# Attention weights by transposes: exponential in transposed form, turned back into PSUM, summed by TensorE

## The chip, the cores and the metric

The kernel runs on one core of one Trainium2 chip. A core has engines that run side by side, each with its own instruction queue, worked off in order: TensorE (PE in the profile; its weight loads are PEld), VectorE (DVE), ScalarE (ACT), GpSimd (POOL) and SyncE (SP). DMA queues move data between DRAM and the on-chip memory SBUF. TensorE writes its results to PSUM, a second on-chip memory [...]. An engine waits for another by a semaphore. The metric is the device time of one execution in microseconds.

## The reference, cut to what matters

Four layers of a graph network over 2048 nodes, 8 batch entries and 128 features, with a sparse adjacency matrix (about 16 neighbours a node). Layers 0 and 1 are attention with 8 heads of 16 features:

```
Q, K, V = (h @ Wq, h @ Wk, h @ Wv) split in heads
scores = einsum('bnhd,bmhd->bhnm', Q, K) / sqrt(16)
scores = where(adj == 0, -inf, scores)
attn = softmax(scores, axis=-1)
x = h + (einsum('bhnm,bmhd->bnhd', attn, V) @ Wo + bo)
x = layer_norm(x); x = layer_norm(x + relu(x @ W1 + b1) @ W2 + b2)
```

Layers 2 and 3 are graph attention with scores `leaky_relu(s_i + s_j)` from two vectors, the same mask and softmax, a residual and a layer norm. All is in fp32.

## The kernel before, in words

The nodes are sorted by their number of neighbours and cut into 16 blocks of 128, one node a partition. Block t has room for `CAPS[t]` neighbours, its slots (30 down to 11, 277 in all). Each layer writes a table to DRAM, one row a node, which holds K and V of all 8 batch entries (2048 floats) in layers 0 and 1. For each slot one indirect DMA of POOL (`gather`, L320) fetches for each of the 128 nodes the row of its neighbour into one of six SBUF buffers `kv`. A chunk is two slots in layers 0 and 1 (some have one), 142 chunks a layer. Node lists that are not full have a mask of -1e30 in `lmask`.

`attention_chunk` (L634) is a generator, and each part up to a `yield` is one step:

1. `kk = kk * q` on VectorE (L642), 2048 elements a partition for two slots.
2. VectorE halves the 128 products of each batch entry by adding halves (L647), once or twice (`2 - k // 2 % 2` times), and TensorE adds up the rest into `pair` (L650) with 8 or 4 fp32 matmuls by the identity, each of which runs as two instructions. ScalarE takes the exponential for each slot with the mask as its bias (L655) and puts the 64 weights of the slot (8 batch entries by 8 heads) into the SBUF tile `w`.
3. `vv = vv * w` on VectorE (L661), again 2048 elements.
4. TensorE transposes the products of each slot and batch entry into the accumulator `acc` in PSUM, adding them over the slots (`add_up`, L622, `turn_into`, L327): 8 transposes a slot.

Block 0 has a folded chunk: nodes with more than 28 neighbours put the rest into lists of other partitions, and a matmul with `merge` brings their share back.

When the weights of a block are all there, `sums` adds them over the slots by a tree of VectorE additions (L467 to L471), takes the minimum and maximum for a check on ranges, and the reciprocal (L480). `scales` spreads and transposes the reciprocals, `outputs` (L680) multiplies `acc` by them, and `attention_tail` (L705), once for each half of the batch, runs the output matrix, layer norms, the two-layer network and the next layer's table rows, mostly on TensorE and ScalarE. `general_path` is for inputs that the check on ranges rejects, and is not run here.

The order is written out by hand in `layers` (L1189): every engine gets its instructions in the order in which the Python code makes them, and the framework adds the semaphores that the data and buffers need. One turn of its loop takes chunk i through steps 1 and 2, and chunk i-2 (taken from the list `weighed`) through step 3 and half of step 4; the other half of step 4 comes at the start of the next turn (the list `added`). Three times in a turn `slot` advances the generators of the tails and of the other threads by one step and lets `fetch` issue gathers for which a buffer is free.

`pair` (L168) is one tile of 128 by 512 fp32, one PSUM bank. In layers 2 and 3 it holds the weights of graph attention, which VectorE writes and reads. `misc()` gives one of three other banks.

Of the kernel before, what the change touches and what calls it, by code (L numbers as in the profile page):

```python
# [46 lines left out]
SEG = 128  # L47
BINS = 64

SUM_MIN, SUM_MAX = 1e-25, 1e30  # L50
SCORE_MAX = 80.0


# [31 lines left out]
def sparse_path(ctx: ExitStack, tc: tile.TileContext, ins: dict, out: bass.AP, flag: bass.AP):  # L85
# [19 lines left out]
    def misc():  # L105
        return pm.tile([P, 512], F32, tag="m", name="m")
# [23 lines left out]
    nc.vector.tensor_reduce(  # L130
        group, ident.rearrange("p (g n) -> p g n", n=MANY), axis=AX.X, op=ALU.add
    )
    eps = const.tile([P, 1], F32, name="eps")
    nc.vector.memset(eps, (EPS / D) ** 0.5)
    iota1 = work.tile([P, N], F16, tag="oT", name="iota1", bufs=1)
# [3 lines left out]

    bufs = [const.tile([P, CHUNK], F32, name=f"kv{i}") for i in range(KVB)]  # L140
    turn = [-1]

    def buffer():
        turn[0] += 1
# [3 lines left out]
    kept = [dram.tile([P, B * P], F32, name=f"kept{t}") for t in range(NT)]  # L148
    perm = const.tile([P, NT], I32, name="perm")
    lists = const.tile([P, sum(CAPS)], I32, name="lists")  # L150
    lmask = const.tile([P, sum(CAPS)], F32, name="lmask")
    first = [sum(CAPS[:t]) for t in range(NT)]

    sorted_lists = const.tile([P, BASE + CAPS[1]], I32, name="sorted_lists")
# [172 lines left out]
    def turn_into(dst, src, start):  # L327
        nc.tensor.matmul(  # L328
            dst, src, ident, start=start, stop=True, is_transpose=True, skip_group_check=True
        )  # L330
# [121 lines left out]
    def folded_sums(w, box):  # L452

        columns = w.shape[-1]
        ps = misc()[:, :columns]
        for i in range(FOLD):
            nc.tensor.matmul(ps, merge, w[:, i, :], start=i == 0, stop=i == FOLD - 1)
        box["folded"] = small.tile([P, columns], F32, tag="folded", name="folded", bufs=1)
        nc.scalar.copy(box["folded"], ps)

    def reciprocal_sums(l, t, w, columns, folded):

        sums = small.tile([P, columns], F32, tag="sums", name="sums")
        n = CAPS[t] if t > 0 else BASE
        if l < 2:

            while n > 2:  # L467
                m = -(-n // 2)
                nc.vector.tensor_add(w[:, : n - m, :], w[:, : n - m, :], w[:, m:n, :])
                n = m  # L470
            nc.vector.tensor_add(sums, w[:, 0, :], w[:, 1, :])  # L471
        else:
            nc.vector.tensor_reduce(
                sums, w[:, :n, :].rearrange("p s c -> p c s"), axis=AX.X, op=ALU.add
            )
        if t == 0:
            nc.vector.tensor_add(sums, sums, folded)
        nc.vector.tensor_reduce(dmin[:, l, t : t + 1], sums, axis=AX.X, op=ALU.min)
        nc.vector.tensor_reduce(dmax[:, l, t : t + 1], sums, axis=AX.X, op=ALU.max)
        nc.vector.reciprocal(sums, sums)  # L480
        return sums
# [140 lines left out]
    def add_up(acc, rows, k, n, folded):  # L622

        for i in range(n):
            for b in range(NB):
# [5 lines left out]
                else:  # L631
                    turn_into(acc[:, b, :], rows[:, i, b, :], k + i == 0 and b % 4 == 0)

    def attention_chunk(l, c):  # L634
        box, t, k, ns = c["box"], c["t"], c["k"], c["ns"]
        if k == 0:
            box["acc"] = pacc.tile([P, NB, P], F32, tag="acc", name="acc")
            box["w"] = work.tile([P, max(CAPS), NB * NH], F32, tag="w", name="w")
        acc, w, q = box["acc"], box["w"], box["qf" if c["folded"] else "q"]
        kv = c["buf"].rearrange("p s (b c) -> p s b c", b=NB)  # L640
        kk = kv[:, :, :, :D]
        nc.vector.tensor_mul(kk, kk, q[:, None].to_broadcast([P, ns, NB, D]))  # L642
        yield
        width = D
        for _ in range(2 - k // 2 % 2):
            width //= 2
            nc.vector.tensor_add(kk[:, :, :, :width], kk[:, :, :, :width], kk[:, :, :, width : 2 * width])  # L647
        sc = pair[:, : ns * NB * NH].rearrange("p (s b h) -> p s b h", b=NB, h=NH)
        for j in range(0, width, NH):
            nc.tensor.matmul(  # L650
                sc, ident, kk[:, :, :, j : j + NH], start=j == 0, stop=j + NH == width
            )
        for i in range(ns):
            at = first[t] + k + i
            nc.scalar.activation(  # L655
                w[:, k + i, :], sc[:, i].rearrange("p b h -> p (b h)"), AF.Exp,
                bias=lmask[:, at : at + 1], scale=1.0,
            )
        yield
        vv = kv[:, :, :, D:].rearrange("p s b (j h) -> p (s b) j h", h=NH)  # L660
        nc.vector.tensor_mul(  # L661
            vv, vv,
            w[:, k : k + ns, :].rearrange("p s (b h) -> p (s b) h", h=NH)[:, :, None, :]
            .to_broadcast([P, ns * NB, HD, NH]),
        )
        yield
        if c["folded"]:
            folded_sums(w[:, BASE:, :], box)
        for i in range(ns):
            add_up(acc, kv[:, i : i + 1, :, D:], k + i, 1, c["folded"])  # L670
            yield

    def sums(l, t, box):
        box["r"] = reciprocal_sums(l, t, box["w"], NB * (NH if l < 2 else 1), box.get("folded"))

    def outputs(l, t, box):
        acc, scale = box["acc"], box["scale"]
# [4 lines left out]
    def scales(l, box):  # L682

        box["scale"] = scale = work.tile([P, NB, P], F32, tag="oT", name="scale", bufs=1)
        if l < 2:
            r = box["r"].rearrange("p (b h) -> p b h", h=NH)
            nc.scalar.copy(
                scale.rearrange("p b (j h) -> p b j h", h=NH),
                r[:, :, None, :].to_broadcast([P, NB, HD, NH]),
            )  # L690
            yield
        for i in range(0, NB, 4):
            pt = misc()
# [123 lines left out]
    def gat_tail(l, t, box):  # L817
# [3 lines left out]
        if l == 2:  # L821
            ns = [work.tile([P, 4, D], F32, tag="n", name="n2") for _ in range(2)]
        else:
            n = work.tile([P, max(CAPS), NB * NH], F32, tag="w", name="n")
            n = n.rearrange("p s c -> p (s c)")[:, : B * D].rearrange("p (b d) -> p b d", d=D)
            ns = [n[:, :4, :], n[:, 4:, :]]
        ys = [None, None]
# [68 lines left out]
    def start():  # L896
# [80 lines left out]
            nc.scalar.activation(junk, src, func, accum_out=dst, **kind)  # L977

        def neighbours(t):
            val = work.tile([P, max(CAPS), NB * NH], F32, tag="w", name="val")  # L980
# [12 lines left out]
            return lambda: total(every, AF.Copy, kept_sum[:, t : t + 1])  # L993
# [187 lines left out]
    def chunk(i):  # L1181
        return every[i] if 0 <= i < len(every) else dict(l=None, k=None, last=False, folded=False)

    def go(c, times=1):

        for _ in range(times if c["l"] is not None else 0):
            next(c["run"], None)

    def layers():  # L1189
        threads.append(first_states((0,)))  # L1190
        drain()
# [6 lines left out]
        weighed, added = [], []  # L1198
        for i in range(len(every) + 2):
            c1, c, n1, n2 = (chunk(i + j) for j in range(-1, 3))  # L1200
            while added:
                c2 = added.pop(0)
                go(c2)
                if c2["last"]:
                    threads.append(tail(c2["l"], c2["t"], c2["box"]))
# [20 lines left out]

            if n1["l"] in (2, 3) and n1["folded"]:
                go(n1)
            if c1["l"] in (2, 3) and c1["last"]:
                sums(c1["l"], c1["t"], c1["box"])  # L1230
                threads.append(scales(c1["l"], c1["box"]))
# [3 lines left out]
            slot()  # L1235
            if c["l"] in (0, 1):
                weighed.append(c)
            while weighed and len(weighed) > (2 if c["l"] in (0, 1) else 0):
                c2 = weighed.pop(0)
                if c2["last"]:  # L1240
                    sums(c2["l"], c2["t"], c2["box"])
                    threads.append(scales(c2["l"], c2["box"]))
                go(c2, 2)
                added.append(c2)
            if c1["l"] in (2, 3):
                go(c1, 2)
                if c1["last"]:
# [533 lines left out]
```

## Time and profile before

| | us |
|---|---|
| median of 3 runs (3017.77 to 3019.6) | 3019.43 |
| the profiled execution | 3168.52 |
| its span | 3166.7 |
| DVE busy | 2748.5 |
| PE busy | 2606.0 |
| POOL busy | 1779.9 |
| ACT busy | 1342.0 |

The profiled execution is longer than the runs without a profile, so what is worked out in its time has to be brought to that of the others. The mean granted clock of TensorE was 0.915 of full speed. Layers 0 and 1 run from about 166 us to 2101 us of the span; ahead of them the lists are made and the first table is written, and after them come layers 2 and 3. A row of a group gives the busy time, the mean length of one instruction, and the idle time of its engine just before, with what ended it. In a timeline the first two columns are start and length in us. A matmul's listed mean contains its latency; as matmuls overlap, busy time divided by their number tells the pace.

### The profile page before, as it was taken

How to read it: one execution, taken by the hardware profiler on the slowest of the kernel's cores; microseconds unless marked ns; L12 is line 12 of the kernel's file. 1: busy time of each engine (PE TensorE's matmuls, PEld its weight loads, DVE VectorE, ACT ScalarE, POOL GpSimd, SP SyncE). 2: the span in 40 equal slices, each digit the busy share in tenths (PEclk: the TensorE clock that was granted, in tenths of full speed). 3: DMA queues.
4: the chain of work that ended last, by engine and by line, in shares of the span. 5: the costliest groups of instructions: out<-in, count | busy, mean ns of one | idle time of the engine just before them, and what ended most of it. 6: DMA issues, size and time to landing. Idle time of an engine off the chain costs nothing. (4 is left out here: it accounts for less than half of the span.)

```text
span 3166.7 us, 52148 instructions
## 1 busy us (share of the span) xinstructions
PE 2606.0 (82%) x19258; PEld 2381.0 (75%) x19258; DVE 2748.5 (87%) x2960; ACT 1342.0 (42%) x4895; POOL 1779.9 (56%) x1296
## 2 busy tenths in 40 slices
PE   4766888888899997888898999986787878687786
PEld 3656777777888886777787888885677777577786
DVE  8898999999999988999999999975787876668876
ACT  3511334444445551333443545553444545144354
POOL 0266677588665545455455455554656554666663
PEclk8988899999999998899999999988878888889888
DMA  8688888888888867788888888866988987899994
GB/s 324 247 336 318 308 295 313 318 324 324 323 337 329 324 275 292 257 332 321 308 318 339 316 336 320 316 220 245 362 323 317 353 305 272 331 335 368 362 360 171
DMA packets 200693, 987.63 MB, mean 312 GB/s; under 512 B 31919, under 2 KB 33713, under 8 KB 128437
## 3 DMA queue, kind: packets, MB, share of 16 engines
q0 software_dynamic: 175024, 890.45, 75.9%
q1 hardware_dynamic: 20502, 75.52, 6.3%
q10 hardware_dynamic: 4904, 18.24, 1.5%
q8 instruction: 155, 2.54, 0.3%
q14 instruction: 108, 0.88, 0.1%
HBM read 937.16 MB, written 91.55 MB: 325 GB/s over the span
## 5 line engine op out<-in xcount | busy, mean ns | idle before, releaser
L321 POOL DMA_INDIRECT kv<-table,lists x955 | 1324.4, 1387 | 922.9 <-PE acc L328 579.8
L328 PE MATMUL acc<-ident,kv 128*128 128x128 f32 x8208 | 1091.4, 287 | 208.9 <-DVE kv L661 93.2
L328 PEld LDWEIGHTS acc<-ident,kv 128*128 128x128 f32 x8208 | 991.1, 149 | 306.1 <-issue 149.9
L642 DVE TENSOR_TENSOR kv<-kv,q 128x2048 f32<-128x2048 f32 (+1 forms) x282 | 629.3, 2232 | 63.5 <-DMA kv<-table,lists 25.4
L661 DVE TENSOR_TENSOR kv<-kv,w 128x2048 f32<-128x2048 f32 (+1 forms) x284 | 632.7, 2228 | 0.0
L650 PE MATMUL pair<-kv,ident 128*128 128x128 f32 (+1 forms) x3344 | 449.4, 286 | 145.7 <-issue 66.3
L650 PEld LDWEIGHTS pair<-kv,ident 128*128 128x128 f32 x3344 | 416.4, 199 | 170.0 <-issue 97.8
L799 DVE TENSOR_TENSOR kv<-kv,pair 128x3584 f32<-128x3584 f32 (+1 forms) x150 | 540.1, 3601 | 2.2 <-issue 0.3
L655 ACT ACTIVATE w<-pair,lmask 128x64 f32<-128x64 f32 x554 | 144.7, 311 | 749.6 <-PE pair L650 736.4
L647 DVE TENSOR_TENSOR kv<-kv 128x1024 f32<-128x1024 f32 (+1 forms) x434 | 442.6, 1020 | 14.4
L496 ACT ACTIVATE n<-m,eps 128x128 f32<-128x128 f32 x512 | 181.4, 367 | 305.4 <-PE m L720 160.3
L321 POOL DMA_INDIRECT kv<-table,sorted_lists x153 | 194.5, 1271 | 131.1 <-PE acc L328 49.0
L846 ACT ACTIVATE n<-m,eps 128x128 f32<-128x128 f32 x256 | 90.7, 372 | 354.4 <-remote 125.7
L804 ACT ACTIVATE kv<-kv,ws 128x128 f32<-128x128 f32 x554 | 176.6, 401 | 86.8 <-issue 29.9
L517 POOL DMA_INDIRECT table<-rows,perm x57 | 80.6, 1414 | 136.9 <-ACT score L570 42.4
L754 PE MATMUL m<-w_L_w,hT 128*128 128x128 f32 x1024 | 156.5, 275 | 0.0
L810 DVE TENSOR_TENSOR kv<-kv 128x1024 f32<-128x1024 f32 x75 | 91.5, 1220 | 73.4 <-ACT kv L804 72.5
L503 ACT ACTIVATE n<-m,rs 128x128 f32<-128x128 f32 x512 | 146.5, 377 | 1.1
L680 DVE TENSOR_TENSOR o<-acc,scale 128x512 f32<-128x512 f32 x128 | 82.9, 684 | 63.7 <-PE acc L328 37.3
L754 PEld LDWEIGHTS m<-w_L_w,hT 128*128 128x128 f32 x1024 | 135.3, 193 | 0.0
L335 PE MATMUL m<-ident,n 128*128 128x128 f32 x640 | 116.1, 303 | 22.6 <-ACT kv L804 6.8
L733 PE MATMUL m<-n1T,w_L_gnn_W 128*128 128x512 f32 x256 | 131.5, 597 | 0.6 <-ACT q L608 0.6
(238 smaller groups left out, 3668.3 us busy)
## 6 DMA issues: line engine op xcount, KB each, us to landing
kept<-xT SPq DMA_DIRECT2D x48, 512.0 KB
xT<-kept SPq DMA_DIRECT2D x48, 512.0 KB
kv<-in_adj_dram SPq DMA_DIRECT2D x16, 1024.0 KB
table<-kv ACTq DMA_DIRECT2D x16, 1024.0 KB
kv<-table,lists POOLq DMA_INDIRECT x955
kv<-in_x_nodes_dram SPq DMA_DIRECT2D x16, 512.0 KB
kv<-table,sorted_lists POOLq DMA_INDIRECT x153
found<-cand POOLq DMA_DIRECT2D x16, 64.0 KB
```

The source lines that it names most:

```text
L321: nc.gpsimd.indirect_dma_start(out=dst, out_offset=None, in_=tables[l][:, :], in_offset=bass.IndirectOffsetOnAxis(ap=index, axis=0), bound ...
L328: nc.tensor.matmul(dst, src, ident, start=start, stop=True, is_transpose=True, skip_group_check=True)
L496: nc.scalar.activation(dst[:, i, :], z[:, i, :], AF.Square, bias=eps, scale=D**-0.5, accum_out=ss[:, i : i + 1],)
L503: nc.scalar.mul(dst[:, i, :], z[:, i, :], rs[:, i : i + 1])
L642: nc.vector.tensor_mul(kk, kk, q[:, None].to_broadcast([P, ns, NB, D]))
L647: nc.vector.tensor_add(kk[:, :, :, :width], kk[:, :, :, :width], kk[:, :, :, width : 2 * width])
L650: nc.tensor.matmul(sc, ident, kk[:, :, :, j : j + NH], start=j == 0, stop=j + NH == width)
L655: nc.scalar.activation(w[:, k + i, :], sc[:, i].rearrange("p b h -> p (b h)"), AF.Exp, bias=lmask[:, at : at + 1], scale=1.0,)
L661: nc.vector.tensor_mul(vv, vv, w[:, k : k + ns, :].rearrange("p s (b h) -> p (s b) h", h=NH)[:, :, None, :] .to_broadcast([P, ns * NB, HD, ...
L754: nc.tensor.matmul(y[:, j, :], hT[:, f, j, :], wt["2"][:, f, :], start=False, stop=f == 1, skip_group_check=True,)
L799: nc.vector.tensor_mul(hv[:, :, :nv, :], hv[:, :, :nv, :], wc[:, :, :nv, None].to_broadcast([P, ns, nv, D]))
L804: nc.scalar.mul(hv[:, i, b, :], hv[:, i, b, :], ws[:, i, b - nv : b - nv + 1])
```

## The change

In layers 0 and 1, VectorE folds once in every chunk, and writes the result by feature, with the 64 columns of both slots side by side, into a tile `hk`. TensorE then adds up eight transposes of `hk` in `pair[:, :128]`, so that a score stands with (slot, batch entry, head) in the partition and the node in the column, and adds the mask, now kept in bf16, with one bf16 matmul a slot. ScalarE takes one exponential of 128 by 128 into `eT`. At the start of the next turn TensorE transposes `eT` back into one of two other parts of `pair`, and the multiplication by V reads the weights from there. The sums of the weights are made by TensorE from the kept exponentials (`block_sums`, for up to eight chunks at a time), and the reciprocal becomes an exponential of the negative logarithm on ScalarE. The bounds of the check on ranges are narrower. The order of the turn has the new step at its start; the lag of two chunks between exponential and multiplication by V stays.

```
-    lmask = const.tile([P, sum(CAPS)], F32, name="lmask")
+    lmask = const.tile([P, sum(CAPS)], BF16, name="lmask")
...
-        if l < 2:
-            while n > 2:
-                m = -(-n // 2)
-                nc.vector.tensor_add(w[:, : n - m, :], w[:, : n - m, :], w[:, m:n, :])
-                n = m
-            nc.vector.tensor_add(sums, w[:, 0, :], w[:, 1, :])
...
+    def block_sums(l, t, box, last):
+
+        terms = [(e, fold_slots[: e.shape[0], :]) for e, folded in box["exps"] if not folded]
+        if "partial" in box:
+            terms.append((ident, box["partial"]))
+        if last and t == 0:
+            terms += [(merge, box["wf"][:, i, :]) for i in range(FOLD)]
+        ps = misc()[:, : NB * NH]
+        for i, (a, b) in enumerate(terms):
+            nc.tensor.matmul(
+                ps, a, b, start=i == 0, stop=i + 1 == len(terms), skip_group_check=True
+            )
+        name = "sums" if last else "partial"
+        box[name] = small.tile([P, NB * NH], F32, tag=name, name=name)
+        nc.scalar.copy(box[name], ps)
+        box["exps"].clear()
+        if last:
+            box["r"] = small.tile([P, NB * NH], F32, tag="logs", name="logs", bufs=1)
+            nc.scalar.activation(box["r"], ps, AF.Ln)
+            threads.append(scales(l, box))
...
-        width = D
-        for _ in range(2 - k // 2 % 2):
-            width //= 2
-            nc.vector.tensor_add(kk[:, :, :, :width], kk[:, :, :, :width], kk[:, :, :, width : 2 * width])
-        sc = pair[:, : ns * NB * NH].rearrange("p (s b h) -> p s b h", b=NB, h=NH)
-        for j in range(0, width, NH):
+        m, at = ns * NB * NH, first[t] + k
+        hk = work.tile([P, NH, P], F32, tag="hk", name="hk")[:, :, :m]
+        kj = kk.rearrange("p s b (j h) -> p (s b) j h", h=NH)
+        nc.vector.tensor_add(
+            hk.rearrange("p j (c h) -> p c j h", h=NH), kj[:, :, :NH, :], kj[:, :, NH:, :]
+        )
+        sc = pair[:m, :P]
+        for j in range(NH):
+            turn_into(sc, hk[:, j, :], j == 0)
+        for i in range(ns):
             nc.tensor.matmul(
-                sc, ident, kk[:, :, :, j : j + NH], start=j == 0, stop=j + NH == width
-            )
-        for i in range(ns):
-            at = first[t] + k + i
-            nc.scalar.activation(
-                w[:, k + i, :], sc[:, i].rearrange("p b h -> p (b h)"), AF.Exp,
-                bias=lmask[:, at : at + 1], scale=1.0,
-            )
+                sc[i * NB * NH : (i + 1) * NB * NH, :],
+                lmask[:, at + i : at + i + 1].to_broadcast([P, NB * NH]), ident_bf,
+                start=False, stop=True, skip_group_check=True,
+            )
+        eT = box["eT"][:m, len(box["exps"]) % NH, :]
+        nc.scalar.activation(eT, sc, AF.Exp)
+        box["exps"].append((eT, c["folded"]))
+        yield
+        turns[0] += 1
+        back = P + turns[0] % 2 * P
+        w = pair[:, back : back + m]
+        nc.tensor.matmul(
+            w, eT, ident[:m, :m], start=True, stop=True, is_transpose=True, skip_group_check=True
+        )
...
+        if c["last"] or len(box["exps"]) == NH:
+            block_sums(l, t, box, c["last"])
         yield
         vv = kv[:, :, :, D:].rearrange("p s b (j h) -> p (s b) j h", h=NH)
         nc.vector.tensor_mul(
             vv, vv,
-            w[:, k : k + ns, :].rearrange("p s (b h) -> p (s b) h", h=NH)[:, :, None, :]
+            w.rearrange("p (s b h) -> p (s b) h", b=NB, h=NH)[:, :, None, :]
             .to_broadcast([P, ns * NB, HD, NH]),
         )
...
-            nc.scalar.copy(
+            nc.scalar.activation(
                 scale.rearrange("p b (j h) -> p b j h", h=NH),
-                r[:, :, None, :].to_broadcast([P, NB, HD, NH]),
+                r[:, :, None, :].to_broadcast([P, NB, HD, NH]), AF.Exp, scale=-1.0,
             )
...
+            for c2 in weighed[-1:]:
+                go(c2)
             while added:
                 c2 = added.pop(0)
                 go(c2)
```

More of the change, by code (lines that the diff above doesn't have):

```diff
@@ L48 @@
 BINS = 64
-SUM_MIN, SUM_MAX = 1e-25, 1e30
+SUM_MIN, SUM_MAX = 1e-15, 1e15
 SCORE_MAX = 80.0
@@ L132, in sparse_path @@
     )
+    fold_slots = const.tile([P, NB * NH], F32, name="fold_slots")
+    nc.vector.tensor_add(fold_slots, ident[:, : NB * NH], ident[:, NB * NH :])
     eps = const.tile([P, 1], F32, name="eps")
@@ L141, in sparse_path @@
     turn = [-1]
+    turns = [0]
     def buffer():
@@ L464, in reciprocal_sums @@
         n = CAPS[t] if t > 0 else BASE
-        if l < 2:
-            while n > 2:
-                m = -(-n // 2)
-                nc.vector.tensor_add(w[:, : n - m, :], w[:, : n - m, :], w[:, m:n, :])
-                n = m
-            nc.vector.tensor_add(sums, w[:, 0, :], w[:, 1, :])
-        else:
-            nc.vector.tensor_reduce(
-                sums, w[:, :n, :].rearrange("p s c -> p c s"), axis=AX.X, op=ALU.add
-            )
+        nc.vector.tensor_reduce(
+            sums, w[:, :n, :].rearrange("p s c -> p c s"), axis=AX.X, op=ALU.add
+        )
         if t == 0:
@@ L637, in attention_chunk @@
             box["acc"] = pacc.tile([P, NB, P], F32, tag="acc", name="acc")
-            box["w"] = work.tile([P, max(CAPS), NB * NH], F32, tag="w", name="w")
-        acc, w, q = box["acc"], box["w"], box["qf" if c["folded"] else "q"]
+            box["eT"] = work.tile([P, NH, P], F32, tag="w", name="eT")
+            box["exps"] = []
+        acc, q = box["acc"], box["qf" if c["folded"] else "q"]
         kv = c["buf"].rearrange("p s (b c) -> p s b c", b=NB)
@@ L643, in attention_chunk @@
         yield
-        width = D
-        for _ in range(2 - k // 2 % 2):
-            width //= 2
-            nc.vector.tensor_add(kk[:, :, :, :width], kk[:, :, :, :width], kk[:, :, :, width : 2 * width])
-        sc = pair[:, : ns * NB * NH].rearrange("p (s b h) -> p s b h", b=NB, h=NH)
-        for j in range(0, width, NH):
+        m, at = ns * NB * NH, first[t] + k
[8 more added lines that the diff above has]
+        for i in range(ns):
             nc.tensor.matmul(
-                sc, ident, kk[:, :, :, j : j + NH], start=j == 0, stop=j + NH == width
-            )
-        for i in range(ns):
-            at = first[t] + k + i
-            nc.scalar.activation(
-                w[:, k + i, :], sc[:, i].rearrange("p b h -> p (b h)"), AF.Exp,
-                bias=lmask[:, at : at + 1], scale=1.0,
-            )
+                sc[i * NB * NH : (i + 1) * NB * NH, :],
+                lmask[:, at + i : at + i + 1].to_broadcast([P, NB * NH]), ident_bf,
+                start=False, stop=True, skip_group_check=True,
+            )
+        eT = box["eT"][:m, len(box["exps"]) % NH, :]
[8 more added lines that the diff above has]
+        )
+        if c["folded"]:
+            box["wf"] = small.tile([P, FOLD, NB * NH], F32, tag="wf", name="wf", bufs=1)
+            nc.scalar.copy(box["wf"].rearrange("p s c -> p (s c)"), w)
+        if c["last"] or len(box["exps"]) == NH:
+            block_sums(l, t, box, c["last"])
         yield
@@ L666, in attention_chunk @@
         yield
-        if c["folded"]:
-            folded_sums(w[:, BASE:, :], box)
         for i in range(ns):
@@ L673, in sums @@
     def sums(l, t, box):
-        box["r"] = reciprocal_sums(l, t, box["w"], NB * (NH if l < 2 else 1), box.get("folded"))
+        if l < 2:
+            nc.vector.tensor_reduce(dmin[:, l, t : t + 1], box["sums"], axis=AX.X, op=ALU.min)
+            nc.vector.tensor_reduce(dmax[:, l, t : t + 1], box["sums"], axis=AX.X, op=ALU.max)
+            return
+        box["r"] = reciprocal_sums(l, t, box["w"], NB, box.get("folded"))
     def outputs(l, t, box):
@@ L823, in gat_tail @@
         else:
-            n = work.tile([P, max(CAPS), NB * NH], F32, tag="w", name="n")
+            n = work.tile([P, NH, P], F32, tag="w", name="n")
             n = n.rearrange("p s c -> p (s c)")[:, : B * D].rearrange("p (b d) -> p b d", d=D)
@@ L979, in neighbours @@
         def neighbours(t):
-            val = work.tile([P, max(CAPS), NB * NH], F32, tag="w", name="val")
+            val = work.tile([P, NH, P], F32, tag="w", name="val")
             val = val.rearrange("p s c -> p (s c)").bitcast(F16)[:, :N]
@@ L1187, in go, with weigh @@
             next(c["run"], None)
+    def weigh(some, added):
+        for c2 in some:
+            if c2["last"]:
+                sums(c2["l"], c2["t"], c2["box"])
+            go(c2, 2)
+            added.append(c2)
     def layers():
@@ L1228, in layers @@
                 go(n1)
+            if c["l"] not in (0, 1) and weighed:
+                weigh(weighed, added)
+                weighed = []
             if c1["l"] in (2, 3) and c1["last"]:
@@ L1237, in layers @@
                 weighed.append(c)
[L1238 to L1244, printed above, removed]
+            if len(weighed) > 2:
+                weigh(weighed[:1], added)
+                weighed.pop(0)
             if c1["l"] in (2, 3):
```

## The prediction

> **What bounds the kernel now.** I began with the page's busy shares and its forty slices, then asked for the busy time of each engine by stage, because layers 0 and 1 (the only ones that run the changed code) may have another limit than layers 2 and 3.
>
> ```profile
> PE 2606.0 (82%) x19258; PEld 2381.0 (75%) x19258; DVE 2748.5 (87%) x2960; ACT 1342.0 (42%) x4895; POOL 1779.9 (56%) x1296
> ...
> DVE  8898999999999988999999999975787876668876
> ```
>
> ```profile
> 166.00:2101.00 1935.00, 1674.32 (x12839) 1538.64 (x12837) 1824.76 (x1504) 809.63 (x2906) 1146.09 (x680) 0.95 0.84 313
> 2101.00:3166.70 1065.70, 824.41 (x5901) 758.16 (x5901) 783.19 (x918) 461.78 (x1825) 604.85 (x579) 0.85 0.86 315
> ```
>
> In the second fence the columns are stage, its length, busy time of PE, PE's weight loads, DVE, ACT and POOL, granted PE clock, DMA share and GB/s. The attention stage lasts 1935 us. DVE is busy 94% of it, PE 87%, DMA 84%: DVE sets the pace, with two others close behind. It handles 284 chunks (142 a layer, 14 of them with one slot, the rest with two), so one takes 6.81 us. The groups of that stage say where DVE's time goes (busy us, mean ns, idle before):
>
> ```profile
> L661 DVE TENSOR_TENSOR kv<-kv,w 128x2048 f32<-128x2048 f32 x270 | 616.5, 2283 | 0.0
> L642 DVE TENSOR_TENSOR kv<-kv,q 128x2048 f32<-128x2048 f32 x268 | 612.3, 2285 | 63.5 <-DMA kv<-table,lists 25.4 <-DMA kv<-table,sorted_lists 16.7 <-ACT q L608 10.1
> L647 DVE TENSOR_TENSOR kv<-kv 128x1024 f32<-128x1024 f32 x270 | 330.5, 1224 | 8.8
> L647 DVE TENSOR_TENSOR kv<-kv 128x512 f32<-128x512 f32 x158 | 109.6, 693 | 5.4
> ```
>
> Idle before the value multiplication L661 is 0.0: DVE never waits for the weights. The timeline shows why:
>
> ```profile
> 305.43 0.69 DVE L647 TENSOR_TENSOR kv<-kv 128x512 f32<-128x512 f32 x1
> ...
> 306.22 1.13 PE L650 MATMUL pair<-kv,ident 128*128 128x128 f32 x8 [1.77 <-ACT rs L487]
> ...
> 306.48 2.28 DVE L661 TENSOR_TENSOR kv<-kv,w 128x2048 f32<-128x2048 f32 x1
> 307.39 0.52 ACT L655 ACTIVATE w<-pair,lmask 128x64 f32<-128x64 f32 x2 [1.79 <-PE pair L650]
> ...
> 308.82 1.97 PE L328 MATMUL acc<-ident,kv 128*128 128x128 f32 x8 [1.47 <-DVE kv L661]
> ...
> 314.81 1.04 PE L328 MATMUL acc<-ident,kv 128*128 128x128 f32 x8
> ```
>
> After the last fold of chunk i, PE adds the scores and ACT takes the exponential, ending at 307.91; yet L661 started at 306.48, because it serves chunk i-2, whose weights lay ready in SBUF. Scores and exponential hang behind DVE, not in its way. The chain of waits says the same from the other side (total us, times, longest):
>
> ```profile
> ACT w L655 <- PE pair L650: 736.4, 276, 12.9
> PE acc L328 <- DVE kv L661: 93.2, 82, 3.2
> ```
>
> [...] the mostly transposing stage of layers 2 and 3 has clock 0.85 at 77% busy, attention 0.95, and the same eight transposes take 1.04 or 1.97 us in the lines above.
>
> **The change part by part.** All in the attention stage; everything else keeps its 3167 - 1935 us.
>
> *DVE loses* the 512 and 256 wide folds (109.6 + 2.5 us), the tree of sums (50.7 + 7.2 + 0.5) and the reciprocal (17.7): 188 us busy, about 175 of time, as consecutive DVE rows overlap by some 80 ns. The remaining fold writes eight-element runs into `hk` at 512-byte steps; no row shows such a write. I take the 1224 ns of L647; [...] at twice that it would add 1.2 us a chunk. Reading `w` from PSUM costs nothing: L799, which reads its weights from `pair`, takes 3887 ns for 3584 elements, the SBUF rate.
>
> *PE* loses L650, 428.0 + 21.3 = 449 us. It gains 284 x 8 score transposes at 132 ns (580.2 us / 4384 of L328) = 300; 554 mask matmuls in bf16, between 50 and 204 ns each (the latter is the mean of the 128x64 bf16 row of `places`), taken as 100 = 55; 284 transposes back = 37; and about 300 fp32 sum matmuls with 64 columns, two instructions each at 121 ns (21.3 us / 176) = 73. That is 465: PE gains nothing.
>
> *ACT*: one 128x128 exponential (377 ns as L503) replaces two of 128x64 (0.52 us together). About 50 copies and logarithms at 0.2 us, and an exponential in place of the copy in `scales`, hide in its idle time (44% busy, and less needed than before); without cover some 20 us. *DMA, POOL, SP*: the same gathers in the same order, no transfer added. Masks in bf16, constants and buffer sizes cost no time.
>
> *The added wait.* `pair` is one PSUM bank. It now holds the scores that PE writes and ACT reads, and beside them the turned-back weights that DVE reads. In the built instruction order L693, the value multiplication of chunk i-2, waits for the ScalarE semaphore value set by the exponential of chunk i, the latest reader of the bank. Two chunks of lag are gone as far as DVE is concerned: K product(i), fold(i), score transposes(i), masks(i), exponential(i), value product(i-2), K product(i+1) are one chain. Behind the waiting L693 stand all of DVE's next chunk, PE's `add_up`, and through it POOL's gathers into that buffer. One two-slot turn of this chain, from the timeline: K product 2.31 (start to start with its fold), fold 1.23, to PE 0.05, eight transposes 1.10, two masks 0.2, to ACT 0.04, exponential 0.37, back to DVE 0.05, value product 2.20: 7.55 us, against 5.67 to 6.38 in the same stretch before. With 14 chunks of about 4.6 the mean is 7.40.
>
> On top come three things. (a) DVE's other work: `outputs` 40.5, minima and maxima 13.7, lists about 35: 0.33 us a chunk, a third of which falls into the new stall; 0.22. (b) PE in its order. After the value product it must do two groups of `add_up` (1.04 each) and the transpose back (0.13), 2.2 us, plus the tail steps recorded between, before the next scores; DVE needs 3.5 for K product and fold, so up to 1.3 us of tail hide. PE's tail work is 1674 - 580 - 449 = 645 us, 20 us a block of 9 chunks, in lumps of up to 3 us (24 matmul instructions of line 754 and 749), in about six of the nine turns. Laying a block's steps over the three slots gives 4 to 9 us of lateness a block, according to the slot where they fall; I take 6.7, or 0.75 a chunk. (c) The clock: with PE less busy and its score matmuls turned into transposes I expect layers 2 and 3's 0.85 rather than 0.95, about 0.6 us on the 5 us of PE in the chain wherever PE binds, which is less than half the time: 0.25.
>
> 7.40 + 0.22 + 0.75 + 0.25 = 8.62 us. 284 x 8.62 = 2448, and about 40 us of DMA and transition waits stay: 2488 for the stage, 553 more than 1935. The profiled execution took 3168.5 us where the median is 3019.4, a ratio of 0.953, which I apply to the difference: +527, 3546 us.
>
> **The rivals.** *R1, the bare chain:* PE keeps up and the clock holds. 7.40 + 0.22 + about 0.2 = 7.8 us; 284 x 7.8 + 40 = 2255, +320, scaled +305: 3325 us. For it: PE falls to 75% busy, so its lateness can drain. Against: the lumps come at fixed places of the order. *R2, a cold PE:* if most transposes run at 1.97 us per eight, `add_up` alone takes 4.2 us after each value product, past DVE's 3.5, and the scores 0.9 more: over 9.4 us a chunk, some 9.6: +831, scaled +792, 3810 us. For it: the 1.97 line after an idle of 1.47. [...] *R3, faster:* the stall is covered and DVE's 175 us count in full: 3019 - 0.953 x 175 = 2853; as PE's 1690 us would then stand in a stage of 1760, up to some 2930. The wait decides unless DVE had over 1.8 us of other work queued between fold and value product in every chunk; it has about 0.1. That the wait does not act at all is the same rival, and it stands in the built order.
>
> **How the numbers follow.** Forecast (8.2 to 9.4 us a chunk, 3430 to 3760 us) 0.52; R1 (below 8.2) 0.28; R2 0.17; R3 0.03, with a sliver at no change. A range of 3290 to 3770 leaves out R3, the lowest fifth of R1 and most of R2. A measurement here tells 0.2% from no change; slower 0.97, faster 0.02, same 0.01.
>
> **What would show it.** Right: idle before the value product L693 of about 2.5 to 3 us a chunk, released by ACT's exponential L677; DVE near 65% busy in the stage; PE busy about as before in a longer stage, at a clock below 0.9; DMA near 245 GB/s there (606 MB in 2488 us); layers 2 and 3 unchanged. Of the terms, (b) shows as ACT waiting for PE's score or mask matmuls later than 1.4 us after the fold's end, and the fold's price in its own row. Wrong: no idle before L693, or a release by an exponential two chunks back; a fold of 2.4 us would put the loss on the strided write instead.

## The result and the profile after

The changed kernel takes 3525.8 us (median of 4 runs, 3525.0 to 3526.6) where the kernel before takes 3019.5 us: a ratio of 1.1675, with a 95% interval of 1.1655 to 1.1695. It is slower by 506 us; forecast were 527.

One thing has to be known to compare the profiles. Layers 2 and 3, which the change does not touch, last about 1050 us in some of the profiles of this study and about 935 us in others, whatever the kernel, and with them the kernel before takes 3141 to 3144 us or 3017 to 3020 us. All runs of a set on one chip agree in it, so it seems to go by the chip; what else ran beside them is not on record, and the cause is open. The profile of the kernel before has the long form (1065 us), the profile of the change the short one (935 us). So kernels are compared by the length of the attention stage, which hardly depends on it (the change has 2419 us in the short form and 2416 in the long one), and by their ratio to the kernel before on the same chip. The kernel before was profiled once, in an execution that is longer than all its 39 others on chips with the long form (3168.5 us, the others at most 3160.9), so its 1931 us of attention may be some 20 us too long.

The page of the changed kernel, busy shares and DVE's slices:

```profile
PE 2759.6 (78%) x19620; PEld 2465.8 (70%) x19620; DVE 2589.0 (73%) x2633; ACT 1295.9 (37%) x4705; POOL 1478.9 (42%) x1296
...
DVE  8877677776766766766666666666667999769997
```

DVE falls to six or seven tenths through the attention slices and comes back to nine only in layers 2 and 3. The attention stage, in the answer by stage (stage, length, busy time of PE, PE's weight loads, DVE, ACT and POOL, PE clock, DMA share, GB/s):

```profile
166.00:2588.00 2422.00, 1893.00 (x13173) 1658.78 (x13174) 1663.11 (x1169) 761.88 (x2710) 846.13 (x684) 0.89 0.70 251
2588.00:3523.00 935.00, 759.85 (x5928) 724.00 (x5927) 784.00 (x920) 462.35 (x1829) 602.53 (x574) 0.89 0.91 357
```

DVE's work fell from 1825 to 1663 us, as the change intends, and its share from 94% to 69%. The time is in its waits. From the groups of the stage (busy us, mean ns, idle before), and last the row of L693 on the page, which takes in the one-slot chunks:

```profile
L693 DVE TENSOR_TENSOR kv<-kv,pair 128x2048 f32<-128x2048 f32 x270 | 617.9, 2288 | 716.8 <-ACT eT L677 714.0 <-PE pair L683 2.7
L659 DVE TENSOR_TENSOR kv<-kv,q 128x2048 f32<-128x2048 f32 x268 | 612.3, 2285 | 2.9 <-DMA kv<-table,lists 2.9
L664 DVE TENSOR_TENSOR hk<-kv 128x1024 f32<-128x1024 f32 x270 | 330.7, 1225 | 8.9
...
L693 DVE TENSOR_TENSOR kv<-kv,pair 128x2048 f32<-128x2048 f32 (+1 forms) x284 | 635.0, 2236 | 743.3 <-ACT eT L677 740.4
```

The value product L693 had no idle time before it; now it has 743 us, released by the exponential L677. The fold with its steps of 512 bytes costs 1225 ns, what the plain one cost, and the product that reads PSUM 2288 against 2283 ns. The timeline of one turn on the three engines, from the K product to the next one:

```profile
812.77 2.28 DVE L659 TENSOR_TENSOR kv<-kv,q 128x2048 f32<-128x2048 f32 x1
...
812.91 1.09 PE L331 MATMUL acc<-ident,kv 128*128 128x128 f32 x8 [2.11 <-DVE kv L693]
...
814.39 1.04 PE L331 MATMUL acc<-ident,kv 128*128 128x128 f32 x8
...
815.09 1.23 DVE L664 TENSOR_TENSOR hk<-kv 128x1024 f32<-128x1024 f32 x1
...
816.38 1.09 PE L331 MATMUL pair<-ident,hk 128*128 128x128 f32 x8 [0.95 <-DVE hk L664]
817.40 0.25 PE L671 MATMUL pair<-ident_bf,lmask 128*64 128x128 bf16 x2
...
817.68 0.28 ACT L677 ACTIVATE eT<-pair 128x128 f32<-128x128 f32 x1 [2.61 <-PE pair L671]
818.00 2.29 DVE L693 TENSOR_TENSOR kv<-kv,pair 128x2048 f32<-128x2048 f32 x1 [1.68 <-ACT eT L677]
...
820.20 2.28 DVE L659 TENSOR_TENSOR kv<-kv,q 128x2048 f32<-128x2048 f32 x1
```

One turn is 820.20 - 812.77 = 7.43 us, each step started by the end of the one before it, on three changes of engine: VectorE to TensorE, TensorE to ScalarE, and ScalarE back to VectorE. This is the bare chain. The waits of the whole program (total us, times, longest) show who stands behind it:

```profile
POOL kv L324 <- PE acc L331: 1289.5, 466, 8.2
ACT eT L677 <- PE pair L671: 818.8, 226, 12.4
DVE kv L693 <- ACT eT L677: 740.4, 280, 7.1
```

PE waits for L693 with its `add_up`, and POOL's gathers wait for PE.

I took the wait apart for each of the 284 chunks, from the times of the trace: from the fold's end to the first score transpose 1.09 us in the mean (median 0.55, a tenth above 2.8), scores and masks 1.35 (1.21 at the shortest), to the exponential 0.07, the exponential 0.28, to the value product 0.07 (median 0.03). The sum is 2.85 us; without PE's lateness, by which is meant the first of these terms, it would be about 1.8. VectorE is idle for 2.62 us of it, as some of its other work falls into this time.

### The profile page after: what moved, and what is told of

It is laid out like the page before. It is cut to its first block, busy times and chain, and to the rows that moved or that the text cites. A ratio compares the mean times of both kernels' runs of the same rounds, so it can differ in the third digit from the quotient of the medians.

```text
span 3523.3 us, 52422 instructions
## 1 busy us (share of the span) xinstructions
PE 2759.6 (78%) x19620; PEld 2465.8 (70%) x19620; DVE 2589.0 (73%) x2633; ACT 1295.9 (37%) x4705; POOL 1478.9 (42%) x1296
## 4 chain that ended last, share of the span: by engine, by line
PE 53%; DVE 22%; DMA 8%; issue 8%; ACT 5%; POOL 0%; POOLq 0%; DVEq 0%; ACTq 0%
PE acc L331 19%; DVE kv L693 10%; PE pair L331 8%; DMA kv<-table,lists 7%; DVE kv L659 5%; PE m L788 3%; DVE hk L664 3%; DVE kv L833 2%; PE m L638 2%; PE m L750 2%; PE m L754 2%; PE m L338 2%; PE m L767 2%; ACT eT L677 2%; PE m L783 2%
## 5 line engine op out<-in xcount | busy, mean ns | idle before, releaser
L324 POOL DMA_INDIRECT kv<-table,lists x955 | 1122.8, 1176 | 1527.2 <-PE acc L331 1199.5
L331 PE MATMUL acc<-ident,kv 128*128 128x128 f32 x8208 | 1170.5, 300 | 527.6 <-DVE kv L693 443.9
L331 PEld LDWEIGHTS acc<-ident,kv 128*128 128x128 f32 x8208 | 1044.9, 156 | 621.5 <-DVE kv L693 506.9
L693 DVE TENSOR_TENSOR kv<-kv,pair 128x2048 f32<-128x2048 f32 (+1 forms) x284 | 635.0, 2236 | 743.3 <-ACT eT L677 740.4
L331 PE MATMUL pair<-ident,hk 128*128 128x128 f32 (+1 forms) x2272 | 330.5, 293 | 68.8 <-DVE hk L664 65.9
L677 ACT ACTIVATE eT<-pair 128x128 f32<-128x128 f32 (+1 forms) x284 | 79.0, 278 | 821.4 <-PE pair L671 818.8
L331 PEld LDWEIGHTS pair<-ident,hk 128*128 128x128 f32 (+1 forms) x2272 | 281.8, 152 | 97.4 <-DVE hk L664 90.6
L664 DVE TENSOR_TENSOR hk<-kv 128x1024 f32<-128x1024 f32 (+1 forms) x284 | 340.4, 1198 | 9.3
L754 PE MATMUL m<-w_L_o,o 128*128 128x128 f32 x512 | 120.2, 324 | 0.0
L772 ACT ACTIVATE hT<-m,w_L_col 128x512 f32<-128x512 f32 x128 | 89.3, 697 | 69.4 <-PE m L767 69.4
```

What stands on the lines that cost most here:

```text
L324: nc.gpsimd.indirect_dma_start(out=dst, out_offset=None, in_=tables[l][:, :], in_offset=bass.IndirectOffsetOnAxis(ap=index, axis=0), bound ...
L331: nc.tensor.matmul(dst, src, ident, start=start, stop=True, is_transpose=True, skip_group_check=True)
L664: nc.vector.tensor_add(hk.rearrange("p j (c h) -> p c j h", h=NH), kj[:, :, :NH, :], kj[:, :, NH:, :])
L693: nc.vector.tensor_mul(vv, vv, w.rearrange("p (s b h) -> p (s b) h", b=NB, h=NH)[:, :, None, :] .to_broadcast([P, ns * NB, HD, NH]),)
L754: nc.tensor.matmul(z[:, j, :], oT[:, j, :], wt["o"], start=False, stop=True, skip_group_check=True)
```

## The experiments

The theory: the value product of chunk i-2 now waits for the exponential of chunk i, because its weights lie in the bank of the scores; this puts scores and exponential into DVE's way. Its rival: the transposes themselves cost the time, through PE's order or its clock. All whole-program medians come with the ratio to the kernel before on the same chip.

**The weights copied to SBUF.** ScalarE copies the turned-back weights, so that VectorE leaves the bank; all else stays.

```
+        ws = small.tile([P, P], F32, tag="wsb", name="wsb", bufs=2)[:, :m]
+        nc.scalar.copy(ws, w)
+        w = ws
```

> The change with one addition: ScalarE copies the turned-back weights from PSUM into SBUF, and the value product reads them there, so VectorE reads nothing in the bank of the scores. Theory (the wait of the value product for the exponential of the chunk two ahead makes the loss): idle before the value product falls from 743 us to under 100, VectorE's 175 us of saved work come through in part, and the whole takes 2860 to 2960 us, less than the kernel before. Rival (the transposes cost the time, through TensorE's order or its clock): 3300 us or more, TensorE's idle turned into lateness of the scores. Rival (the strided write of the fold): no change from 3526, but its row already shows 1225 ns.

It took 3129.8 us, 0.9975 of the kernel before (0.9958 to 0.9992). Attention fell from 2419 to 1906 us. The groups of its stage:

```profile
L696 DVE TENSOR_TENSOR kv<-kv,wsb 128x2048 f32<-128x2048 f32 (+1 forms) x284 | 634.2, 2233 | 34.5 <-ACT wsb L687 30.2 <-ACT rs L481 3.3 <-issue 0.8
L659 DVE TENSOR_TENSOR kv<-kv,q 128x2048 f32<-128x2048 f32 (+1 forms) x282 | 630.3, 2235 | 161.1 <-DMA kv<-table,lists 106.3 <-ACT q L603 30.1 <-DMA kv<-table,sorted_lists 24.1
```

The wait is gone (34.5 us), and with it the whole loss, though every transpose is still there and ScalarE has more to do. The rival falls. The expected gain did not come: 11 us of the whole program by the medians, 26 of attention by the two profiles, where DVE has some 170 us less to do. It now waits 130 us for gathers.

**Another order.** K product, value product of i-2, transpose back of i-1, and then fold and scores; the bank stays shared.

```
-            for c2 in weighed[-1:]:
-                go(c2)
...
             go(c)
+            if len(weighed) > 1:
+                weigh(weighed[:1], added)
+                weighed.pop(0)
+            for c2 in weighed[-1:]:
+                go(c2)
             slot()
             go(c)
...
-            if len(weighed) > 2:
-                weigh(weighed[:1], added)
-                weighed.pop(0)
```

> The change with another order in the turn of attention: K product of chunk i, value product of chunk i-2, then the transpose back of i-1, then fold and scores of chunk i. The bank is still shared and the semaphores still guard it, but the value product now comes a whole K product after the last exponential. Theory of the wait: idle before the value product falls to 50 to 200 us (what is left is TensorE's lateness), total 2880 to 3080 us. Rival that the bank itself slows TensorE or VectorE: 3300 us or more, since all the accesses are still there.

3240.8 us, 1.031 (1.028 to 1.035), where the expectation had a gain or 2% of loss at most; attention 2028 us. From the waits of DVE:

```profile
DVE kv L693 <- ACT eT L677: 313.3, 166, 6.7
```

Four fifths of the loss go by order alone, with all the accesses to the bank in place. The idle time, 337 us with smaller causes, was more than the 200 us expected: the fold's end to the first score transpose takes 1.6 us in the mean here, and what is later than the K product's cover shows.

**The wait alone, in the kernel before.** A copy of one element a partition of the newest exponential, ahead of each value product.

```
+    newest = [None]
...
+        newest[0] = w[:, k + ns - 1, :1]
         yield
         vv = kv[:, :, :, D:].rearrange("p s b (j h) -> p (s b) j h", h=NH)
+        probe = small.tile([P, 1], F32, tag="probe", name="probe")
+        nc.vector.tensor_copy(probe, newest[0])
```

> The kernel before with the wait alone: ahead of each value product VectorE copies one element a partition of the newest exponential, that of the chunk two ahead, and so waits for it. Nothing else of the change is in it. Theory of the wait: the chain of a chunk becomes 2.31 + 1.23 or 1.95 of folds + 1.1 or 1.97 of scores + 0.52 + 2.20 and about 0.3 between, 8.4 us, with VectorE's other work and TensorE's lateness 9.2 to 9.8: 3700 to 3880 us in all, slower than the change itself, whose chain is shorter. Rival that the wait is worth little and the transposes make the loss: under 3200 us.

3773.8 us, 1.2017 (1.1984 to 1.2051), attention 2562 us or 9.02 a chunk, a little under the 9.2 to 9.8 expected.

From the waits:

```profile
DVE probe L664 <- ACT w L656: 666.0, 261, 7.9
```

From the groups:

```profile
L665 DVE TENSOR_TENSOR kv<-kv,w 128x2048 f32<-128x2048 f32 (+1 forms) x284 | 633.2, 2230 | 0.0
```

The product waits for nothing, the copy ahead of it for 666 us. The wait without the change costs as much as the change and more; by the sum in the expectation, this is because two folds and up to sixteen score instructions make the chain longer.

**The change again**, as a base on the chip of the next runs.

> The change itself once more, beside the others on one chip, as a base for them. In the first set the layers 2 and 3 of every kernel took about 1050 us, as in the profile of the kernel before, where the profile of the change had 936 us; the attention stage had 2419 us. Expected: attention 2400 to 2440 us again on whatever chip, as the chain does not depend on DMA there; the whole 3500 to 3540 us if layers 2 and 3 take 936, or 3620 to 3670 us if they take 1050.

3644.7 us, 1.1601 (1.1562 to 1.164); attention 2416 us, layers 2 and 3 1056 us. Attention stays, the rest moves, as expected: what differs between chips is outside the changed stage.

**Where PE's lateness comes from: tail steps moved.** The first slot of the turn, ahead of the scores, is put behind them.

```
             go(c)
-            slot()
+            if c["l"] not in (0, 1):
+                slot()
             go(c)
             slot()
             if c["l"] in (0, 1):
+                slot()
                 weighed.append(c)
```

> The change with the tails' first slot of each attention turn moved from ahead of the scores to behind them, where TensorE has the exponential and the value product (2.6 us) as cover. Theory (1.1 us a chunk beyond the bare chain is TensorE's lateness from tail steps recorded between value product and next scores): a third to a half of these 320 us goes, 3360 to 3430 us. Rival (the time beyond the bare chain is the slower TensorE clock or ScalarE's queue): 3500 us or more.

3617.7 us; attention 2385 us, 31 us less than the change instead of 100 to 160, with the lateness at 1.09 us as before. A miss: two steps in a row can outlast the value product, and `add_up` is late instead. From the value product's end to the first `add_up` transpose it takes 0.71 us in the mean, where the change has 0.35, so the place of the slots mostly moves the lateness.

**The two-layer network left out** of the attention tails of the change; steps and layer norms stay.

```
...
-            nc.tensor.matmul(
-                ph, wt["1"][:, f * P : (f + 1) * P], n1T.rearrange("p b c -> p (b c)"),
-                start=True, stop=True,
-            )
             yield
-            nc.scalar.activation(
-                hT[:, f].rearrange("p b c -> p (b c)"), ph, AF.Relu,
-                bias=wt["col"][:, 4 + f : 5 + f], scale=1.0,
-            )
...
-            for f in range(2):
-                nc.tensor.matmul(
-                    y[:, j, :], hT[:, f, j, :], wt["2"][:, f, :], start=False, stop=f == 1,
-                    skip_group_check=True,
-                )
```

> The change with the two-layer network left out of the attention tails (no W1 and W2 matmuls, no relu; the steps and the layer norms stay), which takes about 280 us of TensorE work out of the attention stage. Theory (the 1.09 us between fold and first score transpose is TensorE still at tail steps): this lateness falls to 0.3 to 0.6 us, the wait of 2.80 us a chunk to 1.9 to 2.3, attention from 2419 to 2200 to 2300 us. Rival (the lateness is the add_up transposes at a slow clock): no fall, or a rise with a lower clock, attention above 2380 us.

Attention 2378 us (3594.0 in all), the lateness 0.93 us: a sixth less, not half. Another miss, and the stage is about as long as the rival had it (above 2380): the granted clock of the stage fell to 0.87, and `add_up`, with the same number of transposes, took 717 us instead of 689. The trace of the change shows what PE does between the end of a value product and the next first score transpose. Of 309 us of lateness in all, 200 lie in 70 chunks that are over 2 us late. In these PE spends 2.2 us on `add_up`, 1.2 on the output projection with its residual (L750, L754), 0.8 on the block sums (L638) and about 0.5 on the two-layer network.

The clock has a part in it. In the trace's record the granted clock is either full or half: in the attention stage of the change it is at half for 543 us (22%), in that of the kernel before for 186 us (10%). The starts of successive `add_up` transposes in the change are about 109 ns apart or, 803 times in 3815, 190 to 240 ns, and 792 of these 803 lie where the record has the half clock. About a fifth of the matmuls in the stretch before the scores follow each other at the doubled distance. As an estimate from these distances, the lateness would be about 0.7 us instead of 1.09 at full pace, and about 0.4 instead of 0.93 with the network left out. So theory and rival both seem to hold in part: with the network left out, PE has 1734 us of work in the stage in place of 1893, and what is left ran slower (`add_up` 717 us for 689). No run tests the clock alone.

**The block sums covered.** The last sums of a block go behind the scores of their turn.

```
-        if c["last"] or len(box["exps"]) == NH:
-            block_sums(l, t, box, c["last"])
+        if not c["last"] and len(box["exps"]) == NH:
+            block_sums(l, t, box, False)
...
             go(c)
+            if c1["l"] in (0, 1) and c1["last"] and "sums" not in c1["box"]:
+                block_sums(c1["l"], c1["t"], c1["box"], True)
             slot()
```

> The change with the last sums of a block (32 of the 48 groups of sum matmuls) moved from the start of the turn to behind the scores of that turn, under the cover of the value product. In the trace of the change these matmuls stand in front of the latest scores (1.0 us of the 3 us and more). Theory that what TensorE does between value product and next scores makes the 1.09 us of lateness, block sums among it: attention 2375 to 2405 us against 2416, lateness 0.95 to 1.05 us. Rival that the sums are harmless there: within 5 us of 2416.

3508.1 us, 1.1628 (1.1601 to 1.1655); attention 2397 us against 2416 to 2419, lateness 1.04. As expected: the sums take part, about 20 us by the 32 groups that moved.

**Where the gain of the copy version goes: two ways to free the buffers earlier.** Both add to the copy version. First a lag of one chunk, with gathers let further ahead.

```
-            if now[1] - now[0] > (4 if now[1] >= KVB and every[now[1] - KVB]["l"] > 1 else 3):
+            if now[1] - now[0] > 4:
...
-            if len(weighed) > 2:
+            if len(weighed) > 1:
```

> The change with the copy to SBUF and with a lag of one chunk in place of two between exponential and value product, and gathers let one chunk further ahead: buffers come free a turn earlier. Theory that the copy version waits for gathers (130 us of idle before the K product) because buffers are held for three turns: these waits fall under 60 us and the whole is 2 to 5% under the kernel before. Rival (TensorE is then late with the weights, as one K product and fold, 3.5 us, must cover add_up, tail steps, transpose back and copy): idle before the value product rises by 150 us or more and the whole is slower than the copy version.

3173.1 us, 1.0108 (1.0064 to 1.0153); attention 1952 us. On the same chip the copy version itself:

> The change with the weights copied to SBUF by ScalarE, once more, as the base of the run with a shorter lag. Theory that DMA now limits it: attention near 1906 us if the chip has the slower layers 2 and 3, and 1780 to 1860 us with a clear gain over the kernel before (2 to 5%) if it has the faster ones.

3124.8 us, 0.9939 (0.991 to 0.9969), attention 1898 us. From the groups of the run with a lag of one:

```profile
L696 DVE TENSOR_TENSOR kv<-kv,wsb 128x2048 f32<-128x2048 f32 (+1 forms) x284 | 635.1, 2236 | 205.7 <-ACT wsb L687 189.5 <-issue 7.0 <-ACT xT L799 3.5
L659 DVE TENSOR_TENSOR kv<-kv,q 128x2048 f32<-128x2048 f32 (+1 forms) x282 | 629.4, 2232 | 11.4 <-DMA kv<-table,lists 8.0 <-issue 2.9 <-DMA kv<-table,sorted_lists 0.5
```

The gathers are in time (11 us), and the weights are late instead (206 us): the rival named ahead holds. Then the lag of two again, with both slots summed in one turn, and from then until the next turn gathers let one chunk further ahead.

```
-            if now[1] - now[0] > (4 if now[1] >= KVB and every[now[1] - KVB]["l"] > 1 else 3):
+            if now[1] - now[0] > (4 if now[1] >= KVB and every[now[1] - KVB]["l"] > 1 else 3 + ahead[0]):
...
-            go(c2, 2)
+            go(c2, 3)
             added.append(c2)
...
+            ahead[0] = 0
...
+                ahead[0] = 1
```

> The change with the copy to SBUF, the lag of two chunks kept, but both slots of a chunk summed into the accumulator in one turn (the second slot's transposes no longer wait for the next turn), and gathers then let one chunk further ahead. It tells whether the copy version's 125 us of waits for gathers come from DMA's rate or from the moment at which a buffer comes free. Free moment: the waits before the K product fall under 60 us, idle before the value product stays under 70 us, the whole is 1.5 to 4% under the kernel before. Rate: the waits stay above 100 us and the whole stays within 0.5 points of the copy version's 0.994 to 0.998.

This came on the chip with the short layers 2 and 3: 3033.9 us against 3017.2, 1.0048 (1.0032 to 1.0063), attention 1932 us, waits for gathers 96 us and for weights 60. Neither expectation fits. Three versions with different lags, leads and chips end at 1898 to 1952 us, and in all of them PE is busy for 1705 to 1724 us. The stage of the copy version, columns as above:

```profile
169.00:2074.00 1905.00, 1705.53 (x13169) 1513.99 (x13170) 1650.26 (x1167) 813.54 (x2992) 1139.37 (x673) 0.96 0.85 316
```

So the next theory was that PE sets their pace.

**PE's work reduced in both kernels.** The two-layer network left out of the copy version and of the kernel before, by the edit shown above.

> The change with the copy to SBUF and without the two-layer network of the attention tails (W1, W2 and the relu left out), some 280 us less of TensorE work in the attention stage. The three copy versions all ended with attention at 1898 to 1952 us, whatever the lag and the gathers' lead, with TensorE 88 to 90% busy. Theory that TensorE, and through its late release of buffers the gathers, now sets their pace, so that VectorE's saved 175 us can't come through: attention falls to 1700 to 1800 us, near VectorE's 1650 us of work. Rival that DMA's rate sets it (314 GB/s in all three): no more than 30 us less than 1900.

> The kernel before without the two-layer network of the attention tails, as the counterpart of the run above. VectorE has 1825 us of work in its attention stage, so less TensorE work helps it little: attention 1860 to 1910 us against 1931. If TensorE's pace mattered as much there, it would fall as far as the copy version does.

The copy version's attention falls to 1774 us (0.9527 of the whole kernel before, 0.9483 to 0.9571), that of the kernel before to 1880 (0.9841, 0.9803 to 0.988). The same window of both, the copy version first (it takes in 55 us of layer 2 there; the stage of the other ends 50 us later):

```profile
169.00:2000.00 1831.00, 1565.28 (x12206) 1415.71 (x12207) 1681.34 (x1202) 768.04 (x2980) 1142.59 (x698) 0.94 0.89 337
```

```profile
169.00:2000.00 1831.00, 1463.65 (x11298) 1357.87 (x11299) 1774.93 (x1457) 716.21 (x2686) 1099.96 (x662) 0.95 0.87 325
```

The same PE work is worth 124 to 132 us in the copy version and 51 us in the kernel before. With PE relieved, DMA moves 337 GB/s where it moved 316, so its rate was not what held the copy version. VectorE's saved work is real: with the network left out of both, the copy version's attention is 106 us shorter than that of the kernel before. But PE stands close behind VectorE, and the change takes nothing off PE; so in the full kernel PE takes over as the pace. Two things stay open. The edit also takes some 70 us of work off ScalarE, which is busy for 43% of the copy version's stage and is the less likely limit, but was not tested alone; and 77 us of waits for gathers are left with PE relieved.

No version beats both kernels clearly: the copy version is 0.2 to 0.6% ahead on one chip, and a close relative of it 0.5% behind on the other. A PSUM bank of its own for the turned-back weights was not tried.

## Why the prediction was right

**The wait.** The chain was named before it was measured, and it holds: 743 us of idle before L693 (2.62 a chunk, forecast 2.5 to 3), released by L677; removed by the copy, mostly removed by order, reproduced in the kernel before. The copy run shows that the guard on this one bank was the price: with the weights read from SBUF the idle time is 34.5 us, and attention takes 1906 us in place of 2419. Why the guard goes by the bank and not by the columns is not shown by any run.

**The terms.** The bare chain was put at 7.55 us for two slots and is 7.43, the most common turn of the trace. The exponential was over-priced, 0.37 for 0.28, by taking a row with another kind of operand. PE's lateness was put at 0.75 and the clock at 0.25, 1.00 together; measured are 1.04 of lateness beyond the handover and 0.13 in the scores, where PE ran below full pace. By the estimate from the distances, some 0.4 of the lateness is the clock's as well, so the tail term was put too high (0.75 for about 0.6) and the clock's at half (0.25 for about 0.5); that their sum nearly fits is in part luck. The mean turn is 8.52 us, forecast 8.62, and the 40 us of DMA and transition waits kept on top were too many: waits for gathers before the K product are 2.9 us in all.

**Where the working was off, though the sum came out.** (b) named lumps of the two-layer network as the cause of the lateness; the trace shows more of the output projection and of the block sums, which the forecast had priced as PE work (73 us; L638 shows about 91) but not placed in the chain. Of these two a run tested only the sums. And the ratio of 0.953 between profile and median was applied to the difference. Of that excess of 149 us, 130 lay in layers 2 and 3 (1065 against 935), which the change does not touch, so nothing should have been scaled: +553 for the stage stands against 2419 - 1931 = 488 in the two profiles and 506 in the medians. The stage was overestimated by 47 to 65 us, and the scaling took 26 of them back, which is luck.

**PE's work** was put at 465 us in place of 449, so that PE would be busy about as before; it is busy for 1893 us of the stage where it was for 1674. The rows show 315.9 + 14.5 for the score transposes, 71 for masks, 87 for the transposes back and 91 for sums, 580 in all. `add_up`, which the change leaves alone, rose from 580 to 689 us. A part of it goes with the lower clock: 98 of 545 `add_up` groups took over 1.8 us, against 26 of 545 in the kernel before, and at some 0.9 us more for each that is an estimated 65 of the 109 us. Another part is the price of one: a transpose back, which stands alone, took 306 ns (L683, 82.5 us / 270) and a mask matmul 129 (71.3 us / 554), where the forecast had 132 and 100. For its lower bound of 50 ns for a mask matmul, the closest that the kernel before shows is two bf16 matmuls of `places` with starts 54 ns apart. In the copy version, at clock 0.96, PE is busy for 1706 us against 1674 before. The clock came out at 0.89, between the 0.95 before and the 0.85 forecast. The forecast took 0.85 from layers 2 and 3 as what transposes bring; but in the profile of the change the same layers have 0.89 with the same instructions, so the share of transposes does not fix it.

**The rivals.** The bare chain (R1, 7.8 us) was missed by 0.7 us of PE lateness, the slow transposes (R2, over 9.4) came only in part: 98 of 545 groups over 1.8 us. R3, the whole 175 us as gain, was wrong twice: the wait acts, and without it the copy version gains only 11 and 20 us by the medians of two sets.

## What to carry to other kernels

Putting two uses into one PSUM bank joined the engines that touch it here, even at separate columns (740 us of waits of the value product for the exponential): before moving an operand there, follow the latest accessor of the bank, not the producer of the data. A lag of two chunks in the pipeline protected the value product only as long as no shared buffer tied the old chunk to the newest one: idle before it was 0.0 us in the kernel before and 743 us in the change. A copy out of the bank took the whole loss away here (34.5 us idle), and an order in which the consumer comes well after the latest accessor took four fifths of it (337 us idle). And where a second engine is nearly as busy as the bound, work taken from the bound alone may be worth little: here about 174 us of work gave 11 to 20 us.

## What the runs showed of the hardware

The exponential of 128 columns without a per-partition operand took 278 ns, less than the one of 64 columns with a bias column in SBUF (314 ns, median). The fold that writes runs of eight elements at steps of 512 bytes took 1225 ns, the plain one of the same size 1224.

Data moved at up to 412 GB/s in a slice of layers 2 and 3 in the profile of the change, at most at 368 in that of the kernel before and at 371 in that of the copy version. With the two lengths of these layers goes a difference of 4% in the median of the kernel before (3141 to 3144 against 3017 to 3020 us). In the traces of the kernel before and of the change, the 4160-byte packets of these layers took 180.5 or 168.6 ns in the mean, with a median of 161 in both, so only some packets were slower.

The half pace came for a minority of transposes. Of the groups of eight `add_up` transposes in the attention stage that run without a break, 98 of 545 took over 1.8 us in the change and 26 of 545 in the kernel before; 384 and 505 took 1.03 to 1.10 us. With the network left out it was 128 of 568, more groups than the 554 of attention, so some are of layer 2.
